# Second attention of a two-layer network: batch 0's lane without its seven idle steps

## The chip, the cores and the metric

The kernel runs on one core of one Trainium2 chip. The metric is the device time of one execution in microseconds (us). Before the change the median of 3 runs is 1161.17 us (1160.54 to 1163.57). The core has a matrix engine (PE, with weight loads listed apart as PEld), a vector engine (DVE), a scalar engine (ACT), a general engine (POOL) and a queue engine that only issues transfers (SP). Each takes its instructions in the order in which the kernel wrote them.

## What is computed

Two transformer layers over x of 8 batches x 512 tokens x 256 features, all in float32, each with an attention part and a feed-forward part, both modulated by a small vector per batch. The change lies in the second layer's attention, a causal linear attention over 16 heads of 16 features:

```
h = layernorm(x) * (1 + ca) + sa
q, k, v = split(h @ qkv_w + qkv_b)          # 16 heads of 16
q' = elu(q) + 1 ;  k' = elu(k) + 1
context_t = q'_t . cumsum_t(k' v^T)          # per head
norm_t    = q'_t . cumsum_t(k')
x = x + ga * ((context / (norm + 1e-6)) @ out_w + out_b)
```

Ahead of it stands the first layer's feed-forward part, in which 16 experts each take 64 chosen tokens of every batch through three 256x256 layers and add the result back into x by index. Behind it stands the second layer's feed-forward part (called the coupling here): three cycles of a small network over four pairs of batches.

## The kernel before

**Lanes and steps.** The kernel is written as Python generators ("lanes"). `Steps.run` calls each lane in turn; what a lane writes between two `yield`s is one step, and all five engines keep the written order (`manual_schedule`). A step in which a lane writes nothing takes no time on the chip: it only shifts the order between lanes. The lanes around the change advance every second round of the scheduler. Within a round, lanes of rank 2 (the second attention's batches, the older batch first) come ahead of rank 3 (the coupling's preparation, `Coupling.ahead`) and rank 4 (the experts, `experts_side`).

**The second attention** is one lane for each of the 8 batches, `batch(b)`, whose first part is `projections(b)`. `steps.start_every(34, batch, 2)` starts a batch every 34 rounds, which is 17 steps of a lane. Counting the steps of a batch's own lane from 0, the places before the change are, for every batch:

| step | what is written | engine and lines |
|---|---|---|
| 0, 1 | mean and variance of x | DVE L1331, L1332 |
| 2 | reciprocal deviation and offset | POOL L1336 to L1340 |
| 4, 5 | normalised x (`xh`) | ACT L1344 |
| 6 to 12 | nothing: `idle(7)`, L1350 | |
| 13 | `hT`: 8 transposes, 2 evictions | PE L279, ACT L284 |
| 23 to 26 | four products k, k, q, q; exp and up; elu; first running sum | PE L1358, ACT L1362 and L1364, DVE L1368, L1391 |
| 27, 28 | values | PE L1375, DVE L1380 |
| 29 | second running sum | DVE L1391 |
| 31, 32 | running sums times q (`k_sums`) | POOL L1415 |
| 33 | wait for the experts' end; gate row; k transposed (`k_tok`) | SP L305, PE L1438, ACT L1441 |
| 36 | normaliser r | PE L1451, DVE L1456, L1457 |
| 37, 38 | states | PE L1466, DVE L1474 |
| 39 | r spread over heads, qn | PE L1490, DVE L1494 |
| 40 | `qz`, four instructions; gated output weight | POOL L1501, DVE L312, L314 |
| 43 to 46 | `am` of the four 128-token chunks: 16 matmuls, 4 evictions and 1 mask each | PE L1520, DVE L1528, ACT L1532, POOL L1534 |
| 47 | bias into x | POOL L1540 |
| 48, 49 | attention output | PE L1547, L1554, ACT L1560 |
| 51, 52 | output projection, sum into x | PE L1568, DVE L1574 |

Batch b+1 is always 17 steps behind batch b, so in the run of batches the four products and the values of one batch (its steps 23 to 28) are written among steps 40 to 45 of the batch in front of it.

**The experts** run as 32 items of two steps each, (a) and (b). Item i writes in step (a): the gather of item i+3 (POOL L1103), the weighting of item i-2 (ACT L1195), the first layer (PE L1159, DVE L1166), the transposes of item i+1 (PE L1148, copied by ACT L1152); in step (b): the scatter of item i-2 (two indirect DMAs, POOL L1202), the last layer of item i-1 (PE L1179, DVE L1184) and the second layer (PE L1159, ACT L1168). The loop runs to i = 33 to drain; then `read_back(1)` loads x of batches 4 to 7 (SP L1213) and ("experts",) is marked as past.

**How they meet.** Batch 0's lane is started after item 21; its step 0 falls into step (b) of item 22, so its even step 2m stands ahead of (b) of item 22+m and its odd step 2m-1 ahead of (a) of item 22+m. Step 13 stands at item 29 (a), step 22 at item 33 (b), the last; the experts are marked past during step 23. The coupling's preparation takes ten steps after that and then issues its small weight loads on SP (from step 34 of batch 0's lane).

PSUM, 8 banks of 128x512 float32, is handed out in the written order (`net.mm()`). The chunk step takes four banks at a time:

```python
strips = [net.mm() for _ in range(4)]
for g in range(2):
    for j in range(4):
        rows = slice(32 * j, 32 * j + 32)
        nc.tensor.matmul(strips[j][:, g * 2 * P : (g + 1) * 2 * P],
            kT[rows, g, cols], qz[rows, g, c].rearrange("r p q -> r (p q)"), ...)
```

Its first eight matmuls read `qz` of g = 0 (the first two of the four POOL instructions), the other eight that of g = 1.

Of the kernel before, what the change touches and what calls it, by code (L numbers as in the profile page):

```python
# [373 lines left out]
def all_of(steps):  # L374

    while True:
        try:
            next(steps)
        except StopIteration as end:
            return end.value  # L380
# [872 lines left out]
def layer1_attention(net, steps, ctx):  # L1253
# [66 lines left out]
    def idle(n):  # L1320
        for _ in range(n):
            yield

    def projections(b):


        xt, va = net.x[b], vaug[b % 2]
        st = net.small.tile([P, NT, 6], F32, name="bn_st")
        mv = net.small.tile([P, NT, 2], F32, name="bn_mv")
        for i in range(NT):  # L1330
            nc.vector.bn_stats(st[:, i, :], xt[:, i, :])  # L1331
            nc.vector.bn_aggr(mv[:, i, :], st[:, i, :])  # L1332
            if i % 2 == 1:
                yield
        rstd = net.small.tile([P, NT], F32, name="bn_rstd")
        nc.gpsimd.tensor_scalar(rstd, mv[:, :, 1], LN_EPS, 1.0, ALU.add, ALU.mult)  # L1336
        nc.gpsimd.tensor_tensor(rstd, rstd, net.neghalf, ALU.pow)
        off = net.small.tile([P, NT], F32, name="bn_off")
        nc.gpsimd.tensor_tensor(off, mv[:, :, 0], rstd, ALU.mult)
        nc.gpsimd.tensor_scalar(off, off, -1.0, 1.0, ALU.mult, ALU.mult)  # L1340
        yield from idle(2)
        xh = pool.tile([P, NT, C], F32, name="xh", bufs=1)
        for i in range(NT):
            nc.scalar.activation(  # L1344
                xh[:, i, :], xt[:, i, :], AF.Identity, bias=off[:, i : i + 1],
                scale=rstd[:, i : i + 1],
            )
            if i % 2 == 1:
                yield
        yield from idle(7)  # L1350
        hT = all_of(net.modulated_T_steps(pool, xh, 1, CA, SA, b, 2))
        yield from idle(10)


        def product(n):
            ps = net.mm()
            for k in range(2):
                nc.tensor.matmul(  # L1358
                    ps, w[:, k, n * P : (n + 1) * P], hT[:, k, :], start=(k == 0), stop=(k == 1)
                )  # L1360
            e = pool.tile([P, T], F32, name="exp")
            nc.scalar.activation(e, ps, AF.Exp, bias=bqk[:, n : n + 1])  # L1362
            up = pool.tile([P, T], F32, name="up")
            nc.scalar.activation(up, ps, AF.Identity, bias=bqk1[:, n : n + 1])  # L1364
            return e, up

        def elu(t, g, made):
            nc.vector.scalar_tensor_tensor(t[:, g, :], made[0], 1.0, made[1], ALU.min, ALU.max)  # L1368

        def values(ip):  # L1370
            ps = net.mm()
            for ii in range(2):
                i = 2 * ip + ii
                for k in range(2):
                    nc.tensor.matmul(  # L1375
                        ps[:, ii * C : (ii + 1) * C], hT[:, k, i * P : (i + 1) * P],
                        w[:, k, 2 * C :], start=(k == 0), stop=(k == 1),
                    )
            for ii in range(2):
                nc.vector.tensor_tensor(  # L1380
                    va[:, 2 * ip + ii, :, 0:4:2, :],
                    ps[:, ii * C : (ii + 1) * C].rearrange("p (s a e) -> p s a e", a=2, e=HD),
                    bv.rearrange("p (s a e) -> p s a e", a=2, e=HD), ALU.add,
                )

        kT = pool.tile([P, 2, T], F32, name="k1T")
        qT = pool.tile([P, 2, T], F32, name="q1T")
        sums = pool.tile([P, 2, T], F32, name="k_sums", bufs=1)

        def scan(g):  # L1390
            nc.vector.tensor_tensor_scan(  # L1391
                sums[:, g, :], ones, kT[:, g, :], 0.0, ALU.mult, ALU.add
            )

        made = product(2)
        yield
        elu(kT, 0, made)
        made = product(3)
        yield
        elu(kT, 1, made)  # L1400
        scan(0)
        made = product(0)
        yield
        elu(qT, 0, made)
        made = product(1)
        yield
        elu(qT, 1, made)
        values(0)
        yield
        values(1)  # L1410
        yield
        scan(1)
        yield from idle(2)
        for g in range(2):
            nc.gpsimd.tensor_tensor(sums[:, g, :], sums[:, g, :], qT[:, g, :], ALU.mult)  # L1415
            yield
        return kT, qT, sums

    def batch(b):
        kT, qT, sums = yield from projections(b)  # L1420
        if b == B - 1:
            steps.past.add(("last exponentials",))
# [589 lines left out]
```

## Time and profile before

| what | value |
|---|---|
| median of 3 runs | 1161.17 us (1160.54 to 1163.57) |
| the profiled execution | 1161.49 us, of which the span from first to last instruction is 1159.8 us |
| PE busy | 1084.9 us, 94% of the span |
| DVE, ACT, POOL busy | 735.9, 573.3, 531.5 us |
| mean granted TensorE clock | 0.973 |
| experts in the trace | to about 714 us on PE, to about 729 us on POOL |
| second attention on PE | from 693.18 us (batch 0's `hT`) to about 990 us |

A line of a timeline gives start, duration, engine, line, operation, the tiles written and read, how many instructions were merged, and in brackets how long the engine had been idle before it and what released it. A line of the windows gives for a stretch its length, each engine's busy time and count in the order PE, PEld, DVE, ACT, POOL, then the granted clock, the DMA engines' busy share and GB/s. A line of the waits gives who waited for whom: total us, times, longest.

### The profile page before, as it was taken

Reading aid. Unit: us, or ns where it says so; the run is one execution under the profiler, and the core shown is the slowest. Engines: PE = TensorE matmul, PEld = TensorE weight load, DVE = VectorE, ACT = ScalarE, POOL = GpSimd, SP = SyncE. Lnnn points to the kernel's source line nnn. Section 1 sums busy time; section 2 is a strip of 40 time slices with the busy share of each in tenths; the row PEclk is TensorE's granted clock in tenths of the full one; section 3 lists DMA queues with packets and bytes.
Section 4 is the critical chain, followed back from the end, with each engine's and each line's share of the span. In section 5 each row is a group of like instructions: output and inputs, shape, how many; then the busy total and the mean of one; then the engine's idle time right before and its main releaser. Section 6 shows DMA issues by size and latency. Waiting matters only on the chain. (4 is left out here: it accounts for less than half of the span.)

```text
span 1159.8 us, 20967 instructions
## 1 busy us (share of the span) xinstructions
PE 1084.9 (94%) x8282; PEld 675.1 (58%) x8282; DVE 735.9 (63%) x1444; ACT 573.3 (49%) x1061; POOL 531.5 (46%) x625
## 2 busy tenths in 40 slices
PE   4889999999999999889898989799999999999996
PEld 3545555555555555478676777466776666444433
DVE  3887777777777777622652322767768666766665
ACT  2255666666665657625232243544545543555544
POOL 4413344435353626568777787556545554000000
PEclk9889999999999999989899999899999999999997
DMA  6200010101101011387857944400000000000102
GB/s 208 90 1 1 1 28 25 29 26 29 42 12 50 5 50 44 91 272 208 204 89 186 241 83 61 114 6 6 6 2 6 7 6 2 0 1 19 54 1 73
DMA packets 67970, 69.02 MB, mean 60 GB/s; under 512 B 10216, under 2 KB 64544, under 8 KB 67872
## 3 DMA queue, kind: packets, MB, share of 16 engines
q1 hardware_dynamic: 55024, 49.32, 13.7%
q0 software_dynamic: 12288, 16.79, 8.4%
q8 instruction: 65, 1.06, 0.4%
q10 hardware_dynamic: 560, 1.58, 0.4%
q14 instruction: 33, 0.27, 0.1%
HBM read 46.38 MB, written 21.01 MB: 58 GB/s over the span
## 5 line engine op out<-in xcount | busy, mean ns | idle before, releaser
L815 ACT ACTIVATE e<-mm 128x512 f32<-128x512 f32 x320 | 171.6, 599 | 104.3 <-PE mm L793 90.7
L734 DVE TENSOR_REDUCE pm<-mm 128x4 f32<-128x512 f32 x256 | 162.2, 681 | 50.0 <-PE mm L701 49.0
L691 PE MATMUL mm<-kT,qT 32*128 32x128 f32 (+3 forms) x1024 | 192.3, 471 | 0.6 <-DVE pm L727 0.4
L793 PE MATMUL mm<-qT,kT 32*128 32x128 f32 (+3 forms) x1024 | 177.1, 465 | 0.0
L820 POOL TENSOR_SCALAR_AFFINE_SELECT e<-e 128x512 f32<-128x512 f32 x128 | 86.1, 693 | 186.7 <-ACT e L815 170.2
L1202 POOL DMA_INDIRECT xs<-y,slot x64 | 102.7, 1604 | 35.2 <-issue 11.3
L793 PEld LDWEIGHTS mm<-qT,kT 32*128 32x128 f32 x1024 | 81.5, 184 | 44.7 <-issue 21.0
L691 PEld LDWEIGHTS mm<-kT,qT 32*128 32x128 f32 x1024 | 92.7, 187 | 19.8 <-issue 4.7
L1753 PE MATMUL mm<-g,cn_w 128*128 128x512 f32 x192 | 93.2, 606 | 0.0
L775 PE MATMUL mm<-e,vaug 128*32 128x512 f32 (+3 forms) x1024 | 79.1, 437 | 2.2 <-POOL e L820 2.2
L1103 POOL DMA_INDIRECT tok<-xg,gidx x64 | 63.9, 998 | 19.4 <-issue 14.3
L1534 POOL TENSOR_SCALAR_AFFINE_SELECT am<-am 128x1024 f32<-128x1024 f32 x32 | 45.9, 1435 | 58.1 <-ACT am L1532 58.1
L1166 DVE TENSOR_SCALAR hid<-mm,eb 128x512 f32<-128x512 f32 x32 | 24.0, 750 | 73.0 <-PE mm L1159 73.0
L1168 ACT ACTIVATE hid<-mm,eb 128x512 f32<-128x512 f32 x32 | 22.0, 687 | 91.9 <-PE mm L1159 91.9
L1179 PE MATMUL mm<-ew,hid 128*128 128x256 f32 x256 | 63.9, 395 | 1.1 <-ACT hid L1168 1.1
L1184 DVE SCALAR_TENSOR_TENSOR y<-mm,eb,gb 128x512 f32<-128x512 f32 x32 | 24.0, 750 | 63.5 <-PE mm L1179 63.4
L1159 PE MATMUL mm<-hid,ew 128*128 128x256 f32 x256 | 62.2, 387 | 0.0
L1159 PE MATMUL mm<-tokT,ew 128*128 128x256 f32 x256 | 61.2, 382 | 0.1
L1358 PE MATMUL mm<-hT,w1qkv 128*128 128x512 f32 x128 | 60.9, 618 | 0.0
L1838 DVE SCALAR_TENSOR_TENSOR m<-th,slope,g 128x512 f32<-128x512 f32 x48 | 34.0, 748 | 40.4 <-ACT th L1831 40.4
L701 PEld LDWEIGHTS <-identb 128*128 128x128 bf16 x320 | 18.8, 98 | 64.4 <-issue 57.1
L1753 PEld LDWEIGHTS mm<-g,cn_w 128*128 128x128 f32 x192 | 33.1, 190 | 39.8 <-issue 37.1
(243 smaller groups left out, 2234.2 us busy)
## 6 DMA issues: line engine op xcount, KB each, us to landing
ew<-in_L_ffn_w SPq DMA_DIRECT2D x72, 256.0 KB, 6.8
x<-in_L_attn_x SPq DMA_DIRECT2D x8, 512.0 KB, 7.6
xs<-x SPq DMA_DIRECT2D x8, 512.0 KB, 3.0
xg<-xh SPq DMA_DIRECT2D x8, 512.0 KB, 3.3
x<-xs SPq DMA_DIRECT2D x8, 512.0 KB, 9.2
out<-res SPq DMA_DIRECT2D x16, 256.0 KB, 2.2
ga_row<-gate_a SPq DMA_DIRECT2D x16, 128.0 KB, 3.1
mod_row<-rows SPq DMA_DIRECT2D x16, 128.0 KB, 4.3
```

The lines of the kernel that those rows point to most:

```text
L691: nc.tensor.matmul(strips[j][:, at : at + nk], qT[g][rows_of(j), p, i * P : (i + 1) * P], kT[rows_of(j), p, :nk], start=(n == 0), stop=Fal ...
L734: nc.vector.tensor_reduce(pm[:, j, g, p, first : first + 4], strips[j].rearrange("q (a k) -> q a k", k=P), AX.X, ALU.max,)
L775: nc.tensor.matmul(av[32 * j : 32 * j + 32, c * P :], va[:, c, :], e[:, j, at : at + T - c * P], start=(a == 0), stop=(a == 3), skip_group ...
L793: nc.tensor.matmul(strips[j][:, at : at + T - c * P], kT[rows_of(j), p, c * P : (c + 1) * P], qT[g][rows_of(j), p, c * P :], start=(n == 0 ...
L815: nc.scalar.activation(e[:, j, :], strips[j], AF.Exp, scale=scale)
L820: nc.gpsimd.affine_select(out=own, in_=own, compare_op=ALU.is_ge, fill=0.0, base=0, pattern=[[0, 4], [1, P]], channel_multiplier=-1,)
L1103: self.net.nc.gpsimd.indirect_dma_start(out=tok[:, n, :], out_offset=None, in_=self.net.xg[half], in_offset=bass.IndirectOffsetOnAxis(ap=s ...
L1159: nc.tensor.matmul(ps[:, o * C : (o + 1) * C], w[i][n][:, k, o * P : (o + 1) * P], src[:, k, :], start=(k == 0), stop=(k == 1),)
L1179: nc.tensor.matmul(ps[:, n * C : (n + 1) * C], hid2[i][:, k, n * P : (n + 1) * P], w[i][2][:, k, :], start=(k == 0), stop=(k == 1),)
L1202: nc.gpsimd.indirect_dma_start(out=net.xs[2 * half + n], in_=y[i][:, n, :], in_offset=None, out_offset=bass.IndirectOffsetOnAxis(ap=self.s ...
L1358: nc.tensor.matmul(ps, w[:, k, n * P : (n + 1) * P], hT[:, k, :], start=(k == 0), stop=(k == 1))
L1753: nc.tensor.matmul(ps, self.w1[:, k, o * P : (o + 1) * P], g[k][bb], start=(k == 0), stop=(k == 1),)
```

## The change

`idle(7)` ahead of `hT` stays for batches 1 to 7 and becomes `idle(0)` for batch 0. No instruction is added or removed. Every step of batch 0's lane from 13 on is written seven lane steps (fourteen rounds) earlier; its steps 0 to 5, the other batches, the experts and the coupling keep their rounds.

```diff
@@ -1347,7 +1347,8 @@
             )
             if i % 2 == 1:
                 yield
-        yield from idle(7)
+
+        yield from idle(7 if b else 0)
         hT = all_of(net.modulated_T_steps(pool, xh, 1, CA, SA, b, 2))
         yield from idle(10)
```

## The prediction

> **What bounds the kernel now.** I read the 40 slices first: PE is at 9 tenths nearly throughout, so what counts is where PE stands still, and whether later work makes up for it. Windows around the place (column order: PE, PEld, DVE, ACT, POOL, clock, DMA share, GB/s) show the one thin stretch, at the hand-over from experts to second attention:
>
> ```profile
> 640.00:702.50 62.50, 56.29 (x278) 47.77 (x277) 16.33 (x28) 23.49 (x45) 49.64 (x41) 1.00 0.66 149
> 702.50:714.00 11.50, 10.66 (x51) 9.07 (x50) 4.24 (x11) 3.55 (x7) 7.86 (x6) 1.00 0.52 60
> 726.00:739.00 13.00, 7.32 (x49) 4.68 (x48) 9.54 (x21) 5.34 (x11) 6.51 (x8) 0.74 0.86 224
> 739.00:766.00 27.00, 26.97 (x283) 18.39 (x284) 16.74 (x31) 12.49 (x22) 14.44 (x11) 1.00 0.08 13
> ```
>
> From 739 on PE hardly stops (26.97 of 27.00 here, 179.13 of 180 from 950 to 1130). A microsecond lost before 766 is therefore a microsecond at the end. PE's timeline of the thin stretch:
>
> ```profile
> 712.13 1.99 PE L1179 MATMUL mm<-ew,hid 128*128 128x256 f32 x8 [0.84 <-ACT hid L1168]
> ...
> 724.28 1.04 PE L279 MATMUL mm<-ident,xh 128*128 128x128 f32 x8
> 725.15 0.27 PE L1438 MATMUL mm<-ident,k1T 128*128 128x128 f32 x1
> 725.65 0.76 PE L1438 MATMUL mm<-ident,k1T 128*128 128x128 f32 x5 [0.22 <-DVE k1T L1368]
> 730.08 0.43 PE L1451 MATMUL mm<-k_sums,gather 128*32 128x128 f32 x8 [3.67 <-POOL k_sums L1415]
> 732.51 0.66 PE L1451 MATMUL mm<-k_sums,gather 128*32 128x128 f32 x8 [2.01 <-POOL k_sums L1415]
> 733.10 5.15 PE L1466 MATMUL mm<-v1aug,k_tok 128*128 128x384 f32 x12
> 738.18 0.75 PE L1490 MATMUL mm<-att_r,spread 32*128 32x128 f32 x16
> 738.85 5.42 PE L1358 MATMUL mm<-hT,w1qkv 128*128 128x512 f32 x12
> 744.20 1.15 PE L1520 MATMUL mm<-qz,k1T 32*128 32x256 f32 x16
> ```
>
> Idle here: 0.84 + 0.22 + 3.67 + 2.01 = 6.74 us. L1466 takes 5.15 us where batch 1's takes 2.87: the windows of single microseconds grant 0.50 from 731 to 737, so this drop costs 2.3 us there and 0.3 in L1451. The last two lines matter most: between L1490 and the chunks (L1520) stand three products (L1358) of batch 1, 5.42 us, and POOL makes `qz` behind them. POOL's timeline says why L1451 is late, and how long `qz` takes:
>
> ```profile
> 724.74 1.55 POOL L1202 DMA_INDIRECT xs<-y,slot  x1 [1.08 <-DMA xs<-y,slot]
> 726.71 2.02 POOL L1202 DMA_INDIRECT xs<-y,slot  x1 [0.42 <-ACT exp L1362]
> 728.19 1.84 POOL L1415 TENSOR_TENSOR k_sums<-k_sums,q1T 128x512 f32<-128x512 f32 x1
> 731.20 1.26 POOL L1415 TENSOR_TENSOR k_sums<-k_sums,q1T 128x512 f32<-128x512 f32 x1 [1.17 <-DVE k_sums L1391]
> ...
> 740.44 3.77 POOL L1501 TENSOR_SCALAR qz<-qn,parity 128x512 f32<-128x512 f32 x4 [5.22 <-DMA cn_b<-in_L_ffn_cn_b]
> ```
>
> The experts' scatters hold POOL until 728.19, and the first `k_sums` starts at once. Last, PE's waits from 766 on and the place of the longest wait for `qz`:
>
> ```profile
> PE mm L1520 <- POOL qz L1501: 4.8, 2, 2.4
> ```
>
> ```profile
> 808.71 0.71 PE L1520 MATMUL mm<-qz,k1T 32*128 32x256 f32 x8 [2.40 <-POOL qz L1501]
> 809.35 3.68 PE L1358 MATMUL mm<-hT,w1qkv 128*128 128x512 f32 x4
> ```
>
> So an uncovered `qz` does stop PE, and the clock falls too: L1358 x4 takes 3.68 us there, 1.98 at 938.36.
>
> **The change part by part.** Batch 0's steps s >= 13 go to s-7; the rest stays. By front's counting: `hT` to 6 (item 25 b), products to 16 to 19 (items 30 b to 32 a), values to 20 and 21, `k_sums` to 24 and 25, `k_tok` to 26, r to 29, states to 30 and 31, qn to 32, `qz` to 33, chunks to 36 to 39, outputs to 41 and 42, projection to 44 and 45. Batch 1's `hT` stays at batch 0's step 30, its products at 40 to 43. The experts' mark is set in step 23, so `until` at 26 doesn't hold the lane.
>
> *Batch 0's `hT` (8 PE, 2 ACT) into item 25: nothing.* It comes ahead of L1179 at 669.91. Its `xh` ends near 670.8, so PE waits about 1 us and works 1.04: L1179 slips 1.9 us. The following transposes wait for POOL's gathers (L1148 <- DMA tok: 0.75 at 676.65, 1.21 at 683.70, 0.44 at 702.22): 2.4 us of slack take it up. Without that cover it would cost 1.9. Its absence at 693.18 gives nothing either, since the wait at 702.22 only grows.
>
> *Projections between the experts' last items: -2 us on PE up to `k_tok`.* From 702.5 the same matmuls run, without batch 1's `hT` (1.04) and without the waits of 0.84 and 0.22: values and `k_tok` end near 724.3, not 726.4. ACT's eight evictions (0.57 each) now stand ahead of the weighting of items 29 to 31: the last y goes from 721.6 to about 723.7, and its scatter starts at 724.74. That is covered by 1 us; if not, the scatters slip by the excess. On DVE batch 0's elu and first running sum now stand ahead of half of batch 1's statistics, which end near 714 instead of 709.7; POOL wants them at 717.77.
>
> *r: 1.7 us earlier.* `k_sums` stays behind the last scatter, at 728.19. Both running sums are then done, so two of 1.27 end at 730.75; before, the second ended at 732.46. L1451 ends about 731.45, not 733.17. PE idles 5.3 + 0.9 us meanwhile, and the clock falls as before. Then batch 1's `hT` (1.04) stands among the states: L1490 ends about 0.6 us earlier than before (between 1.4 earlier and 0.4 later, by when the clock comes back).
>
> *The `qz` wait: +4.7.* Nothing is written on PE between steps 32 and 36. From L1490's end qn takes 1.4 us, the first half of `qz` 1.88 plus 0.1 of handing over: 3.4 idle; after eight matmuls (0.57) the second half, 1.88 - 0.57 = 1.3. The 5.42 us that hid this still have to run, later. DVE's gated weight needs the gate row, issued at 732.45 as before (still behind `read_back(1)`, ahead of the coupling's loads); were it late, `qz` covers 3.8 us.
>
> *Chunks alone: +0.4.* Four in a row are held by evictions: the last batch's three take 3.65 us (L1520 x48 at 973.06), 1.22 each against 1.08. Batch 2's offsets on POOL now stand behind `qz` and the first mask, so its `xh` stands late among ACT's chunk copies; product 2 (1.76) on PE covers most. Say 0 to 0.6 in all.
>
> *A second drop of the clock: +2 (0 to 3).* The trace has no 3.4 us `qz` wait. The nearest row is the 2.40 us one, which brought 0.50 for about 4 us and cost 1.7 in L1358. I take 2. The Trainium skill (TensorE: Matmul & The Clock Gate, Part 1) names an idle window of about 3.4 us as what halves the clock; taken literally a wait cut by eight matmuls could escape, and the sum would be 5.9. The 2.40 us row, shorter than that window, speaks against it.
>
> *Batch 1's r: +1.4.* Before, batch 0's chunks, outputs and projection lay between batch 1's values and its r. Now only batch 2's `hT` and `k_tok` (1.0 + 0.8) do, against DVE 0.76 + 1.22 and POOL 1.27 with hand-overs: 1.4 of waiting (0.9 to 1.7). From there the order is as before.
>
> Sum: -0.6 + 4.7 + 0.4 + 2 + 1.4 = +7.9 us. The profiled 1161.49 is 0.3 above the median and has 1.7 outside its span, neither touched: 1161.2 + 7.9 = 1169.1. Likeliest case's own range: -1.4 + 4.7 + 0 + 0 + 0.9 = +4.2 to 0.4 + 4.7 + 0.6 + 3 + 1.7 = +10.4, 1165.4 to 1171.6.
>
> **The rivals.** *The tail pays (faster).* At 702 to 733 projections fill the waits and r is 1.7 earlier; if that also spared the first clock drop (2.6), 4.3 us would be won: 1157. For: 6.74 us of idle lie there. Against: POOL is held by scatters to 728.19, and the `qz` wait alone is 4.7. It decides only if batch 1's products still ran ahead of the chunks. *It evens out.* No second drop, the first spared, batch 1's r covered: -0.6 - 2.6 + 4.7 + 0.4 = +1.9, 1163. Against: PE's wait before r gets no shorter in one piece (5.3). *The experts are upset too.* `hT` in item 25 is not taken up (+1.9) and a late last scatter holds `k_sums` (+1): +10.8, 1172; for it, the 1 us of cover. *The mark holds the lane*, so that only projections move: batch 1's products again hide `qz`, r gains 1.7: 1159.5. Against: mark at 23, lane at 26.
>
> **How the numbers follow.** Forecast 0.73, upset experts 0.12, evens out 0.08, tail pays 0.05, lane held 0.02. Range 1164 to 1172.5: the forecast's range stretched to most of the third case. What a measurement can tell from no change is 0.3%, 3.5 us: slower above 1164.7. The first two cases are slower, 0.85; evening out and the held lane are the same, 0.10; the tail paying is faster, 0.05.
>
> **What would show it.** In the changed profile: L1520's first eight with a wait for `qz` of 3 us or more and the second eight with over 1; L1451 of batch 0 near 731; no wait left before the last L1179; a clock near 0.5 after the `qz` wait; a wait of 1 to 2 us at batch 1's second L1451. A `qz` wait under 1.5 us, or PE's end shifted against the sum of its waits, would make it wrong.

## The result, and the profile after

The changed kernel takes 1166.86 us (median of 6 runs, 1164.99 to 1170.43) against 1160.66 for the kernel before on the same chip: ratio 1.0053, 95% interval 1.0034 to 1.0072, or 6.2 us slower. Measured once more beside other versions it is 1.0043 (1.0027 to 1.0058). The profiled execution took 1167.05 us with a span of 1165.3. The prediction was 1169.1, 7.9 us slower, with a range of 1164 to 1172.5.

The same stretch of PE's timeline as before (start, duration, engine, line, what, count, idle before it). The new line in the file moves every line number behind it by one, so L1451 is now L1452, L1520 is L1521 and so on; where the text compares the two, it uses the number before the change.

```profile
723.55 0.82 PE L1439 MATMUL mm<-ident,k1T 128*128 128x128 f32 x6
730.85 0.66 PE L1452 MATMUL mm<-k_sums,gather 128*32 128x128 f32 x8 [6.47 <-POOL k_sums L1416]
732.07 0.65 PE L1452 MATMUL mm<-k_sums,gather 128*32 128x128 f32 x8 [0.56 <-POOL k_sums L1416]
732.65 2.93 PE L1467 MATMUL mm<-v1aug,k_tok 128*128 128x384 f32 x6
735.37 1.46 PE L279 MATMUL mm<-ident,xh 128*128 128x128 f32 x8
736.66 1.46 PE L1467 MATMUL mm<-v1aug,k_tok 128*128 128x384 f32 x6
738.06 0.75 PE L1491 MATMUL mm<-att_r,spread 32*128 32x128 f32 x16
742.38 0.71 PE L1521 MATMUL mm<-qz,k1T 32*128 32x256 f32 x8 [3.57 <-POOL qz L1502]
743.71 6.34 PE L1521 MATMUL mm<-qz,k1T 32*128 32x256 f32 x56 [0.62 <-POOL qz L1502]
749.98 1.98 PE L1359 MATMUL mm<-hT,w1qkv 128*128 128x512 f32 x4
...
770.97 0.43 PE L1452 MATMUL mm<-k_sums,gather 128*32 128x128 f32 x8
772.84 0.42 PE L1452 MATMUL mm<-k_sums,gather 128*32 128x128 f32 x8 [1.44 <-POOL k_sums L1416]
773.19 2.87 PE L1467 MATMUL mm<-v1aug,k_tok 128*128 128x384 f32 x12
775.99 0.75 PE L1491 MATMUL mm<-att_r,spread 32*128 32x128 f32 x16
```

Batch 1's products (L1359 at 749.98) now stand behind all four chunks. Ahead of the chunks PE waits 3.57 + 0.62 us for `qz`, and batch 1's second half of r waits 1.44 us: the two places that the prediction named. L1490 of batch 0 started at 738.18 before and starts at 738.06 now, so the early work won next to nothing. (Executions also drift ahead of the change. Counted from POOL's scatter behind batch 0's offset, the last one ahead of the moved `hT`, which starts at 668.67 before and at 669.08 now, L1490 comes 0.53 us earlier.) L1490 of batch 1 started at 768.66 and now at 775.99: **from one to the other 30.48 us before, 37.93 after.** I use that distance below, because it is the same within 0.01 us wherever nothing is wrong, while the times of runs spread over several us. It does not see what the change does ahead of batch 0's L1490.

The windows of single microseconds (PE, PEld, DVE, ACT, POOL, then the granted clock) show four edges of the clock in this run:

```profile
729.00:730.00 1.00, 0.00 (x0) 0.00 (x0) 0.00 (x0) 0.00 (x0) 1.00 (x2) 0.70 0.26 38
736.00:737.00 1.00, 1.00 (x9) 0.87 (x8) 0.17 (x1) 0.57 (x1) 0.00 (x0) 0.89 1.04 350
743.00:744.00 1.00, 0.38 (x8) 0.29 (x8) 0.26 (x2) 0.00 (x0) 0.65 (x1) 0.52 0.55 112
749.00:750.00 1.00, 1.00 (x13) 0.40 (x5) 0.72 (x2) 1.00 (x4) 0.93 (x2) 0.56 0.43 85
```

Down at 729.4 (0.70 is 0.40 us at full and 0.60 at half clock), up at 736.2, down again at 743.0 and up at 749.9. The chunks lie almost wholly in the second drop.

POOL's timeline shows why r is hardly earlier: the last scatter and the two `k_sums` behind it.

```profile
726.09 1.55 POOL L1202 DMA_INDIRECT xs<-y,slot  x1 [1.20 <-ACT k_tok L1442]
727.95 1.55 POOL L1202 DMA_INDIRECT xs<-y,slot  x1 [0.30 <-issue]
728.95 3.06 POOL L1416 TENSOR_TENSOR k_sums<-k_sums,q1T 128x512 f32<-128x512 f32 x2
740.32 3.33 POOL L1502 TENSOR_SCALAR qz<-qn,parity 128x512 f32<-128x512 f32 x4 [8.31 <-DMA cn_w<-in_L_ffn_cn_w]
```

### The profile page after: what moved, and what is told of

Its sections match the earlier page's. It is cut to its first block, busy times and chain, and to the rows that moved or that the text cites. A ratio compares the mean times of both kernels' runs of the same rounds, so it can differ in the third digit from the quotient of the medians.

```text
span 1165.3 us, 20965 instructions
## 1 busy us (share of the span) xinstructions
PE 1085.6 (93%) x8282; PEld 678.3 (58%) x8282; DVE 736.1 (63%) x1444; ACT 573.4 (49%) x1061; POOL 528.2 (45%) x625
## 4 chain that ended last, share of the span: by engine, by line
PE 73%; POOL 8%; DMA 7%; DVE 6%; issue 4%; ACT 1%; SPq 0%; POOLq 0%; DVEq 0%; ACTq 0%
PE mm L793 11%; PE mm L1754 7%; PE mm L775 6%; PE mm L691 5%; PE mm L1359 4%; PE mm L701 4%; PE mm L1812 4%; PE mm L1521 3%; DMA tok<-xg,gidx 3%; DMA xs<-y,slot 3%; PE mm L596 3%; PE mm L1159 3%; PE mm L1179 2%; PE mm L874 2%; PE mm L1555 2%
## 5 line engine op out<-in xcount | busy, mean ns | idle before, releaser
L1179 PE MATMUL mm<-ew,hid 128*128 128x256 f32 x256 | 63.5, 393 | 0.0
L1359 PE MATMUL mm<-hT,w1qkv 128*128 128x512 f32 x128 | 59.9, 604 | 0.0
```

Of the source, the lines that this page charges most:

```text
L1179: nc.tensor.matmul(ps[:, n * C : (n + 1) * C], hid2[i][:, k, n * P : (n + 1) * P], w[i][2][:, k, :], start=(k == 0), stop=(k == 1),)
L1359: nc.tensor.matmul(ps, w[:, k, n * P : (n + 1) * P], hT[:, k, :], start=(k == 0), stop=(k == 1))
```

## The experiments

The theory on trial: the moved work behind the projections costs, by the `qz` wait without cover, the clock's drop in it, and batch 1's r without cover; the early part wins next to nothing, because the scatters hold POOL. The rivals: that early `hT` or early projections upset the experts, or that being out of phase costs by itself.

In the table, "distance" is from batch 0's to batch 1's L1490 in the profiled run.

| run | ratio to the kernel before (95%) | median, before (us) | distance (us) |
|---|---|---|---|
| before | | | 30.48 |
| the change | 1.0053 (1.0034 to 1.0072) | 1166.86, 1160.66 | 37.93 |
| the change again | 1.0043 (1.0027 to 1.0058) | 1166.94, 1162.07 | 37.04 |
| `hT` alone early | 1.0002 (0.9990 to 1.0013) | 1161.54, 1161.46 | 30.47 |
| projections alone early | 0.9989 (0.9978 to 0.9999) | 1159.69, 1161.46 | 30.48 |
| the same again | 0.9976 (0.9963 to 0.9988) | 1159.53, 1162.07 | 30.48 |
| one step instead of seven | 1.0020 (1.0007 to 1.0033) | 1164.54, 1161.46 | 32.65 |
| chunks held back | 1.0063 (1.0042 to 1.0084) | 1167.28, 1161.46 | 37.29 |
| from qn on held back | 1.0021 (1.0009 to 1.0032) | 1164.46, 1161.97 | 33.47 |
| chunks held back, `xh` of batch 2 later | 0.9998 (0.9986 to 1.0011) | 1162.23, 1162.07 | 30.48 |
| outputs held back | 1.0038 (1.0022 to 1.0054) | 1165.29, 1161.97 | 35.14 |
| PE kept busy in the wait | 1.0071 (1.0052 to 1.0090) | 1169.54, 1161.97 | 36.11 |
| `qz` on DVE | 1.0050 (1.0028 to 1.0072) | 1169.26, 1161.97 | 39.76 |
| projections early, `k_sums` on DVE | 0.9914 (0.9897 to 0.9932) | 1151.81, 1162.07 | 30.48 |

**`hT` alone early.** The seven idle steps stand behind `hT` instead of ahead of it.

```diff
-        yield from idle(10)
+        yield from idle(10 if b else 17)
```

> Only batch 0's hT is early (item 25 b); the seven idle steps stand behind it instead of ahead of it, so that everything else is at its old place. Theory: no difference, 1160 to 1161 us; PE waits about 1 us for xh ahead of hT and the next waits for gathers shrink by as much. Rival (hT upsets the experts): the last scatter and k_sums on POOL come 1 us or more later, and the time is 1 to 2 us above before.

No difference. The early `hT` is free, and so is its absence from its old place.

**Projections alone early**, run twice.

```diff
         kT, qT, sums = yield from projections(b)
+        if b == 0:
+            yield from idle(7)
```

> The change, with seven idle steps more behind batch 0's projections: hT, the four products, the values and k_sums stay early, k_tok and everything behind it is at its old place. Theory: 1160 to 1161 us like the kernel before, since r still waits for k_sums behind the last scatter (L1451's second half ends about 732.7 us) and batch 1's products again hide qz. Rival (projections among the experts' items cost): about the changed kernel's time, 1165 to 1168.

> The projections alone early, once more, beside the version with k_sums on DVE. Theory: 0 to 1.5 us under the kernel before (0.7 us measured on PE's way to batch 1).

0.11% and 0.24% under the kernel before (1.8 and 2.5 us); both intervals exclude 1, the first one barely. Projections among the experts' last items don't cost, they gain about 2 us, somewhat more than expected. So the whole loss lies behind them, and in the full change it is larger than the 6 us that show.

**One step instead of seven.**

```diff
-        yield from idle(7 if b else 0)
+        yield from idle(7 if b else 6)
```

> idle(6) for batch 0: its lane is one step early instead of seven. Two of batch 1's three products (3.5 us) then still stand ahead of the first chunk, the third behind it. Theory: the first wait for qz shrinks from 3.57 to under 1 us, the second half waits about 1.3 us, the clock keeps 1.00 there, batch 1's r keeps its cover: 1161 to 1163 us. Rival (what counts is that the lanes are out of phase at all, or that work stands among the experts' items): one step is as bad as seven, or a seventh of it.

PE's timeline of this run from the spread of r on:

```profile
739.17 0.75 PE L1491 MATMUL mm<-att_r,spread 32*128 32x128 f32 x16
739.85 3.70 PE L1359 MATMUL mm<-hT,w1qkv 128*128 128x512 f32 x8
743.48 0.71 PE L1521 MATMUL mm<-qz,k1T 32*128 32x256 f32 x8
745.25 0.71 PE L1521 MATMUL mm<-qz,k1T 32*128 32x256 f32 x8 [1.05 <-POOL qz L1502]
```

Two products (3.63 us) cover the first half of `qz` fully and leave 1.05 of the second. Batch 1's spread of r then waits 0.80 for the reciprocal, which I had not foreseen. The distance grows by 2.2, not by a seventh of 7.4 and not by 7.4: what counts is how much of batch 1 still stands ahead of the chunks. The time is 1164.54 us, 3.1 over the kernel before and more than the 1161 to 1163 expected.

**Chunks held back.**

```diff
             steps.past.add(("last normaliser",))
-        yield from idle(3)
+        yield from idle(3 if b else 10)
```

> The change, with batch 0's four chunks and all behind them held at their old places (seven idle steps more ahead of the chunks); projections, k_sums, r, states, qn and qz stay early. Theory (the loss is the qz wait without cover, the clock drop behind it, and batch 1's r without cover; the early part gains almost nothing because the scatters hold POOL): batch 1's products again run between L1490 and the chunks, no wait for qz, no second drop of the clock, no wait at batch 1's r; from batch 0's r on the order is that of before, so batch 1's L1490 lies within 1 us of before and the time is 1160 to 1161 us, 6 us under the changed kernel. Rival (the early projections or the early hT upset the experts, and the waits behind them are only where it shows): the time stays within 2 us of the changed kernel, 1165 to 1168.

A miss: 1167.28, no better than the change. The wait for `qz` was gone, but another stood in its place. PE's timeline of this run:

```profile
737.90 5.42 PE L1359 MATMUL mm<-hT,w1qkv 128*128 128x512 f32 x12
743.25 1.15 PE L1521 MATMUL mm<-qz,k1T 32*128 32x256 f32 x16
744.33 1.98 PE L1359 MATMUL mm<-hT,w1qkv 128*128 128x512 f32 x4
748.23 0.99 PE L1521 MATMUL mm<-qz,k1T 32*128 32x256 f32 x2 [1.92 <-ACT up L1365]
749.38 3.70 PE L1521 MATMUL mm<-qz,k1T 32*128 32x256 f32 x14 [0.15 <-ACT up L1365]
```

and ACT's waits from 735 to 760 (who waited for whom: total, times, longest):

```profile
ACT xh L1344 <- POOL bn_off L1340: 7.9, 1, 7.9
```

With `qz` early, batch 2's offset (L1340) is behind it on POOL, and its statistics are behind qn on DVE. Batch 2's `xh` waits for that offset at the head of ACT's queue, and batch 1's exponentials, whose first three products were finished at 743, wait behind it until 746.94. Their PSUM banks stay full, the second chunk finds none (its matmuls do not read `up`, yet PE is released by it), PE stops for 2.07 us, and in this run the clock is at 0.50 from 748.5 to 755.3.

**From qn on held back.** The same, seven idle steps ahead of `qn` instead of the chunks.

> The changed kernel with seven idle steps ahead of batch 0's qn: projections, k_sums, k_tok, r and states stay early, qn, qz, chunks, outputs and projection are back at their old places, and batch 2's statistics, deviation and offset again stand ahead of qz on DVE and POOL. Theory: the whole loss lies in qn to outputs: batch 1's L1491 within 1 us of before, 1160 to 1161 us. In the run that held back the chunks alone the time stayed at 1167 because batch 2's offset, now behind batch 0's qz on POOL, held batch 2's xh on ACT ahead of batch 1's exponentials, and PE ran out of banks; here that is gone. Rival (the early r and states cost by themselves): 1164 us or more.

A partial miss: 1.0021, distance 33.47. DVE's queue was the reason this time: batch 2's statistics (739.23 to 741.37) stand ahead of qn, which wants to run at 739.3, so `qz` starts at 743.89 and PE waits 0.58 + 0.62 for it; `xh` still holds the exponentials up to 745.79, and a chunk waits 0.59 for DVE's masks. The time, 1164.46, is also what the rival had said (the early r and states cost by themselves); the next run tells the two apart.

**Chunks held back, batch 2's `xh` written later.** On top of the chunks' run; the first hunk stands ahead of `xh`, the second ahead of `hT`:

```diff
-        yield from idle(2)
+        yield from idle(8 if b == 2 else 2)
...
-        yield from idle(7 if b else 0)
+        yield from idle(0 if b == 0 else 1 if b == 2 else 7)
```

> As the run that held back the chunks alone, but batch 2's xh is written six steps later, behind batch 1's exponentials on ACT (its hT stays where it is). Theory: what kept that run slow was batch 2's xh ahead of the exponentials, waiting for an offset that POOL makes behind batch 0's qz; now no wait for qz, none for ACT, no second drop of the clock: from batch 0's spread of r (L1491) to batch 1's 30.5 us as before instead of 37.9, 1160 to 1161.5 us. Rival (the early r, qn and qz cost by themselves): 33 us or more from one to the other, 1163 or more.

```profile
739.54 0.75 PE L1491 MATMUL mm<-att_r,spread 32*128 32x128 f32 x16
740.22 5.42 PE L1359 MATMUL mm<-hT,w1qkv 128*128 128x512 f32 x12
745.57 1.15 PE L1521 MATMUL mm<-qz,k1T 32*128 32x256 f32 x16
746.64 1.98 PE L1359 MATMUL mm<-hT,w1qkv 128*128 128x512 f32 x4
748.55 1.15 PE L1521 MATMUL mm<-qz,k1T 32*128 32x256 f32 x16
```

Distance 30.48, ratio 0.9998: the whole loss against the kernel before is gone, though projections, r, states, qn and `qz` are as early as in the change. That settles both readings: the cover of `qz` and of batch 1's r, and the queue behind `xh`. (Batch 2's later `xh` by itself was not run.) Something is still lost against the projections alone, 1162.23 to 1159.53 us beside the same kernel before, with intervals that lie apart. The place shows in PE's rows: there batch 1's `hT` runs at 721.66, ahead of the wait for `k_sums`; here it runs at 735.87, behind that wait and at half clock, among the states (1.92 us). This was not tested by itself.

**Outputs held back**: seven idle steps ahead of batch 0's bias (L1541).

> The changed kernel with seven idle steps ahead of batch 0's bias, so that only its outputs and its projection are back at their old places (steps 47 to 52), among batch 1's running sums. Theory: batch 1's second wait for k_sums (1.44 us) goes, the qz wait stays: 1.4 us under the changed kernel. Rival: the running sums are late for another reason (POOL), and the wait stays.

The wait at batch 1's r is gone (L1452 x16 in one piece at 770.38). The distance is 2.79 under the change's: 1.44 for that wait, and most of the rest because the second drop of the clock was shorter in this run (the 56 chunk matmuls took 5.24 us, not 6.34). The median, 1165.29 us, is 1.6 under the change's first, as expected but within the spread of the runs.

**PE kept busy in the wait.** Four matmuls that nobody reads, between `qz` and the chunks.

```diff
+        if b == 0:
+            spent = net.mm()
+            for _ in range(4):
+                nc.tensor.matmul(spent, net.ident, ones, start=True, stop=True, ...)
         yield from idle(3)
```

> The changed kernel with four extra matmuls (identity by ones, about 3.5 us of PE, into a bank nobody reads) written between batch 0's qz and its chunks. They do no useful work; they only keep PE busy while it would have waited for qz. Theory (the second drop of the clock is a cost of its own): the first chunk starts when it did, about 742.4 us, but the clock stays at 1.00 and the four chunks take about 1.2 us each instead of 1.6: PE is past the chunks 1 to 2 us earlier, 1165 to 1166 us. Rival (the chunks are held by their evictions, not by the clock): no gain, or a loss where the extra matmuls overrun the wait.

```profile
736.77 3.70 PE L1512 MATMUL mm<-ones,ident 128*128 128x512 f32 x8
740.41 0.71 PE L1525 MATMUL mm<-qz,k1T 32*128 32x256 f32 x8
741.75 4.41 PE L1525 MATMUL mm<-qz,k1T 32*128 32x256 f32 x56 [0.62 <-POOL qz L1502]
```

In this profile the clock stays at 1.00 through the chunks, and they take 4.41 us where the change's took 6.34 and 5.45 in its two profiles; the distance is 36.11 against 37.93 and 37.04. So in the profiles the drop is a cost of its own, 1 to 2 us. (Each matmul of this code is two records of the trace, hence x8 for four.) As a time the gain did not show: the median is 1169.54 us against the 1165 to 1166 expected; of four runs the profiled one (1164.90) was the fastest, the others 1169 to 1172, and I can't say why.

**`qz` on DVE.** `nc.gpsimd.tensor_scalar` becomes `nc.vector.tensor_scalar` for batch 0.

> The changed kernel with batch 0's four qz instructions on DVE instead of POOL, the other batches as they were: the suspected wait made shorter without a change of any step. Theory: the wait of PE ahead of the chunks shrinks from 3.57 + 0.62 to 2 to 3 us by the shorter instructions (DVE's 128x512 products take 0.7 us elsewhere against POOL's 0.83 to 0.94), the clock may or may not drop: 1 to 3 us under the changed kernel. Rival: as long as before.

The wait shrank as expected: 2.48 in one piece instead of 3.57 + 0.62, as four instructions on DVE take 1.67 us against POOL's 3.33. The gain did not come. In this profile the masks on DVE were later (PE waits 1.12 for them), since gated weight and batch 2's statistics now end at 746; and the clock stood at 0.50 from 748.5 to 755.4, over product and outputs too. A shorter wait with the drop in a worse place: the expected 1 to 3 us did not come (1169.26), and as a time the run is inconclusive.

**The change again.**

> The changed kernel once more, for the spread between its runs. Theory (a drop of the clock that may or may not come, worth 1.7 us and more, at two places): 1165 to 1169 us, 0.4 to 0.7% over the kernel before.

4.9 us slower this time, 1.0043; the two intervals overlap.

**Projections early, `k_sums` on DVE.** On top of the projections alone; batch 0's gated weight moves just ahead of its bias, so that DVE does not wait for the gate row. That move by itself was not run.

```diff
-            nc.gpsimd.tensor_tensor(sums[:, g, :], sums[:, g, :], qT[:, g, :], ALU.mult)
+            (nc.gpsimd if b else nc.vector).tensor_tensor(
+                sums[:, g, :], sums[:, g, :], qT[:, g, :], ALU.mult
+            )
```

> Only the projections early (seven idle steps behind them, as in the run of the projections alone), and batch 0's two k_sums products on DVE instead of POOL, with batch 0's gated output weight written just ahead of its bias so that its gate row, issued behind the second read back, holds nothing. Theory (the gap ahead of r is POOL's queue: k_sums behind the last scatters): k_sums are done near 727 us, r's two halves follow k_tok with under 1.5 us of waiting instead of 4.8, the clock keeps 1.00 from 726 to 740, batch 0's L1490 starts near 731 instead of 738, and the time is 6 to 7 us under the kernel before, 1154 to 1156. Rival (something else is late at that place, such as the experts' last item or batch 2's statistics): no more than 2 us under it.

PE's timeline, then POOL's:

```profile
723.98 0.82 PE L1443 MATMUL mm<-ident,k1T 128*128 128x128 f32 x6
724.89 0.43 PE L1456 MATMUL mm<-k_sums,gather 128*32 128x128 f32 x8
725.50 0.43 PE L1456 MATMUL mm<-k_sums,gather 128*32 128x128 f32 x8 [0.18 <-issue]
725.85 2.87 PE L1471 MATMUL mm<-v1aug,k_tok 128*128 128x384 f32 x12
728.89 0.75 PE L1495 MATMUL mm<-att_r,spread 32*128 32x128 f32 x16 [0.17 <-DVE att_r L1462]
729.57 5.42 PE L1359 MATMUL mm<-hT,w1qkv 128*128 128x512 f32 x12
```

```profile
726.57 1.55 POOL L1202 DMA_INDIRECT xs<-y,slot  x1 [0.30 <-issue]
```

The last scatter starts at 726.57, behind both halves of r, which no longer wait for it. From `k_tok` to the spread of r PE needs 4.91 us, in the second run of the projections alone 11.55 (723.47 to 735.02), and the clock is 1.00 throughout. 1151.81 us, 0.86% under the kernel before and 1.3% under the change: the fastest version of all. Of the 7.7 us under the second run of the projections alone, 6.6 are this stretch. The whole gain, 10.3 us, is more than the 6 to 7 expected; some 2 of it are what the projections win by themselves.

## Why the prediction was right, and where its terms were off

The sign, the mechanism and the range held. By its own steps:

- *`hT` into item 25 costs nothing*: right. PE waited 0.59 + 0.16 us for `xh` there, and the run of `hT` alone moved nothing. In the change the clock even fell for 3.4 us there (671.4 to 674.8, L1179 3.07 us instead of 1.99), and later waits for gathers took that up too.
- *PE 2 us earlier up to `k_tok`*: right, 724.37 instead of 726.41.
- *r 1.7 us earlier*: too much; it ended 0.45 earlier (732.72 against 733.17), or, counted from the scatter at 669.08 (668.67 before, 666.21 in the second profile of the change), 0.86 and 1.41 earlier. The last scatter began 0.83 and 0.27 later, counted so, and the two `k_sums` took 3.06 us together where two of 1.27 were assumed, although the prediction's own row shows the first at 1.84. L1490 came 0.12 earlier, counted from the scatter 0.53 and 0.48; the 0.6 of the sum was nearly right.
- *The `qz` wait, +4.7*: 3.57 + 0.62 = 4.19. The four POOL instructions took 3.33 us, not 3.77, and the second half's wait was 0.62, where a sign of the prediction had asked for over 1.
- *Chunks and clock, +0.4 and +2*: together 2.66. The span from the first to the last chunk matmul is 7.60; less the 0.62 of waiting and 4 x 1.08 = 4.32. In the second profile of the change it is about 1.8, so the range of 0 to 3 was right to be wide. In the run with PE kept busy, at full clock, the same span less 0.62 and 4.32 leaves 0.7 for the evictions (0.4 was put); the rest is the clock. The row that the 2 was taken from held 0.50 for 3.4 us, 809.44 to 812.86, not for about 4.
- *Batch 1's r, +1.4*: 1.44, and 0.21 more up to its spread.
- *Not foreseen*: batch 1's products and batch 0's outputs, no longer mixed with the chunks, take 20.99 us from the end of the chunks to batch 1's r where the same work took 22.12. That gives back 1.1, the largest miss of the sum. In PE's rows 0.54 of it lies in the attention output (L1547, L1554) and 0.39 in the values (L1375); why was not tested.

Sum on the way to batch 1: -0.12 + 0.08 + 4.19 + 2.66 + 1.65 - 1.13 = 7.33, which is 775.99 - 768.66; predicted 7.9. (The 0.08 is the spread itself, 0.75 to its end when a wait follows.) The profiled spans differ by only 5.5 us, because at batch 2's `qz` wait, 2.40 us in the kernel before and 2.39 in the changed one, the clock fell in the one run and not in the other: from batch 2's to batch 3's L1490 it is 35.69 us against 33.98. In the second profile of the change it fell there too, 35.64. That 1.7 us is chance and no part of the change. Counted from the scatter ahead of the change, batch 1's L1490 comes 6.92 us later than before, and 6.08 in the second profile; the medians say 6.2 and 4.9.

*The rivals.* The experts were not upset (`hT` and projections alone). "The tail pays" was right in what it saw, 6.7 us of waiting that can be won, and in its condition that batch 1's products must run ahead of the chunks; but it takes `k_sums` off POOL as well. What the prediction passed over in a sentence was batch 2's offset moved behind `qz`: covered in the change, it cost all of the expected gain when only the chunks were put back.

## What to carry to other kernels

Between lanes that share in-order queues, an idle step that writes nothing still decides which work covers which wait: before taking it out, list for each moved instruction what stood beside it on PE and what it now stands ahead of on every other queue. When a wait is put right and the time does not move, look at the next queue (here ACT's `xh` ahead of the exponentials) before giving up the theory. And the gap on the critical engine was won here by moving the work that is late to a queue with room, `k_sums` from POOL to DVE, and not by moving the waiters forward.

## What the runs showed of the hardware

The clock's edges in one run lie on a grid: 729.4, 736.2, 743.0 and 749.9 in the change are 6.8 us apart, twice 3.41. The drop at batch 2's wait in the kernel before lasts 3.42, from 809.44 to 812.86. In each of the 14 profiles all edges between 600 and 1000 us fit one grid of 3.413 us to 0.05 us; only the place of the grid differs from run to run. The 3.41 us between two points of the grid are called a window below. Whether a wait of 2.4 us halves the clock depends on where it falls on that grid. The kernel before, then the change:

```profile
809.00:810.00 1.00, 1.00 (x9) 0.47 (x6) 0.56 (x1) 0.47 (x1) 0.00 (x0) 0.72 0.08 16
812.00:813.00 1.00, 1.00 (x6) 0.04 (x4) 0.75 (x2) 0.00 (x0) 0.29 (x1) 0.57 0.00 0
```

```profile
816.03 0.71 PE L1521 MATMUL mm<-qz,k1T 32*128 32x256 f32 x8 [2.39 <-POOL qz L1502]
817.00:818.00 1.00, 1.00 (x3) 0.38 (x2) 1.00 (x3) 0.92 (x2) 0.00 (x1) 1.00 0.06 16
818.00:819.00 1.00, 1.00 (x10) 0.40 (x12) 1.00 (x3) 0.30 (x1) 1.00 (x1) 1.00 0.00 0
```

In the kernel before the wait fell into one window (806.03 to 809.44), with 1.0 us of matmuls left in it. In the change's first profile it was cut by an edge at 814.7, the two windows held 2.3 and 2.1 us of matmuls, and the clock stayed at 1.00. Over the 14 profiles from 560 to 1000 us, a window at full clock with at most 1.34 us of matmuls was always followed by a drop, and one with more than 2.29 never; between these both happened, so the busy time alone does not decide there.

The prediction weighed the Trainium skill (TensorE: Matmul & The Clock Gate, Part 1), which names free-running windows of about 3.4 us and a whole idle one as the condition; the traces agree on the window and its free run, but a window with about 1.0 us of matmuls in it (806.03 to 809.44 in the kernel before) was enough to fall. Where PE was the limit, a drop was worth 1 to 2.5 us here, and it may account for much of the spread of some 5 us between runs of one kernel; that was not tested by itself.
